# Three graph attention layers: partly filled columns of neighbours packed densely, their indices picked by one-hot products

## The chip, the cores and the metric

The kernel runs on one core of a Trainium2 chip. The metric is the device time of one execution in microseconds (us). The engines are PE (matrix products, with PEld loading weights), DVE (vector), ACT (activations), POOL (here it issues the indirect DMAs) and SP (issues ordinary DMAs, and runs in order). A wait is named by the engine that waits and by what ended it.

## What is computed

There are 6250 nodes with 256 features and 100000 edges from `src` to `dst`. Layers 1 and 2 are attention layers with 4 heads of 64, layer 3 one with 8 heads of 32. For each node the layer looks at the nodes that have an edge to it (and in layers 1 and 2 at the node itself):

```python
# layers 1 and 2 (xl, xr are x @ Wl, x @ Wr per head)
e = leaky_relu(xl[src] + xr[dst], 0.2); logits = einsum('ehc,hc->eh', e, att)
alpha = softmax of logits over the edges of each dst
out = segment_sum(xl[src] * alpha, dst) + b
# layer 3
e = leaky_relu(s1[src] + s2[dst], 0.2); out = segment_sum(softmax(e) * Wh[src], dst)
```

Between layers 1 and 2 stands an elu; behind layers 2 and 3 stand a residual sum and a layer norm.

## The kernel before

**Plan** (`make_plan`, L735): counts the edges of each node, sorts the nodes by degree, writes for each node the list of its sources next to its features to DRAM (`near_d`), and makes layer 1's table xl, one row of 260 numbers per node (`tables`). The lists are built on DVE in halves: `laid`, `shifted`, `filled` for the first nine of 17 segments, then for the other eight. The weights of layer 1 and of layer 2 are prepared here too (`left`, `right`; ACT L829, L833, DVE L842, L846). Seven indirect DMAs into a tile `spare` (L1254) have no reader.

**Blocks and columns.** The sorted nodes form 49 blocks of 128, a node to a partition, the highest degrees first. Block b has `cols[b]` columns: 27 in block 0, 25 in block 1, falling to 9 in block 48, 803 in all. Column j holds the j-th source of each node of the block. `columns` (L53) fixes these counts from the numbers of edges and nodes alone, with a margin, so that a last column may hold few real sources; the other lanes then point to a row "nobody" that weighs nothing. A column costs one indirect DMA on POOL (`gather_rows`, L1438), which brings 128 rows from the layer's table in DRAM into a column of a row tile. A row tile holds nine columns (T); there are nine of them (ROWS), so three blocks at most are in flight. `chunks` cuts a block into two to four row tiles (with a column for the node itself in layers 1 and 2).

**Packs.** Ten last columns share three gathers per layer: the packs are the blocks [3, 13, 17, 36], [26, 40, 47, 48] and [31, 43]. Each block has a fixed range of lanes in its pack. `pick_rows` (L1405, SP) copies the source indices into a column `pick` with small DMAs, `gather_pack` (L1410, POOL) gathers, `lay_rows` (L1418, SP) copies a block's share from the pack's tile into its row tile, and `lack_rows` (L1426, SP) fills the lanes below with nobody's row. So there are 796 gathers of columns and packs in a layer.

**Layers 1 and 2** are one function, `layer2` (L1702). For a block, `attend` computes on DVE z = max(g, xr) (the first chunk is made one block ahead, L1797, the others L1777), z times `at` (L1800), and the sum per head (L1801) into `lg`. `weights` takes the maximum (L1579, once per block, which marks blocks in the trace), the exponentials on ACT (L1587) and the normalisation on DVE. `weighted_sum` multiplies the rows by their weights, the last `few` columns on ACT with four instructions per column (L1629), the others on DVE (L1633), and PE adds the rows up by products with the identity (L1640). A row tile is free once PE has read it. `turns` transposes on PE (L1558, copied by ACT at L1563) and multiplies by weights (`product`, L1568): in layer 1 this makes `pr`, the block's own part for z, whose padding DVE sets at L1884, and the rows of layer 2's tables. `few` is `min(S // 3, last chunk - 1)` in layer 1 and `(2 * S - 2) // 3` in layer 2, with S = cols + 1.

**Order.** `layer2` starts with `begins(0..2)`, `find_few`, `gather(0)`, `turns(0)`, `fetch(1)`, `turns(1)`; then for each block b: `attend(b)`, the end of block b-1, `weighted_sum(b)`, `fetch(b + 2)`, `turns(b + 2)`. `begins(b)` in layer 1 is `start1` (L1887): an indirect DMA on POOL that brings a block's lists and features (`near_r` from `near_d`). `fetch(b)` calls `begins(b + 2)`; where block b + 2 opens a pack, it also calls `begins` of all the pack's blocks, and one block later `pick_rows`. With the packs above, four of these are at block 1 (3, 13, 17, 36). Then come the block's gathers, in order, on POOL. The order is written by hand; each engine runs its instructions in this order.

**Layer 3** is a loop behind them: per block, DVE alone computes `lg` (L2010), the weights, the products (L1662) and their sum (L1674). The gathers of block b + 1 are issued ahead of block b, and the result goes out by an indirect DMA on POOL (L2040).

Of the kernel before, what the change touches and what calls it, by code (L numbers as in the profile page):

```python
# [36 lines left out]
P = 128  # L37
# [10 lines left out]
def columns(E, N, NB):  # L48

    mean = E / N
    pmf = [math.exp(-mean)]
    for k in range(1, 200):
        pmf.append(pmf[-1] * mean / k)
    over, sd = [], []
    for c in range(199):
        p = sum(pmf[c + 1 :])  # L60
        g = sum((k - mean) * pmf[k] for k in range(c + 1, 200))
        over.append(N * p)
        sd.append(math.sqrt(max(N * (p * (1.0 - p) - g * g / mean), 0.0)))
    cols = []
    for b in range(NB):
        most = P * b
        cols.append(next(
            c for c in range(199) if (over[c] + 3.5 * sd[c] <= most if b else over[c] < 0.01)
        ))
    low = max((c for c in range(199) if N - over[c] <= P // 4), default=0)  # L70
    high = next(c for c in range(199) if over[c] <= P // 4)
    pmf += [0.0] * 200
    held = next(
        c for c in range(199)
        if N * sum((k - c) * pmf[k] for k in range(c, 200))
        + 3.5 * math.sqrt(N * sum((k - c) ** 2 * pmf[k] for k in range(c, 200))) <= P
    )
    assert cols[1] <= held < cols[0]
    part = {}
    for b in range(len(EARLY), NB):  # L80
        c = cols[b] - 1
        n = max(8, -(-int(math.ceil(over[c] + 3.5 * sd[c] - P * b)) // 8) * 8)
        if n < P:
            part[b] = n
    packs, taken = [], set()
    for b in sorted(part):
        if b in taken or part[b] > P * 3 // 4:
            continue
        pack, at = [], 0
        for k in range(b, NB):  # L90
            if k in part and k not in taken and at + part[k] <= P:
                pack.append((k, at, part[k]))
                at += part[k]
        if len(pack) > 1:
            packs.append(pack)
            taken.update(k for k, _, _ in pack)
    return cols, low, high, held, packs
# [569 lines left out]
def kernel(  # L667
# [22 lines left out]
    cols, low, high, held, packs = columns(E, N, NB)  # L690
# [7 lines left out]
    node_i = plan.tile([P, NB], I32, name="node_i")  # L698
    fits = plan.tile([P, 1], I32, name="fits")
# [11 lines left out]
    with tc.manual_schedule():  # L711
        make_plan(
            tc, x, src, dst, ((wl1, wr1, att1), (wl2, wr2, att2)), (b1, b2), w3, a3,
            cols, low, high, held, packs, node_i, fits, ident, eps, nobody, att, wc, wh, fixed, xl1_d,
            near_d,
# [6 lines left out]
    with tc.If(ok != 0):  # L722
        with tc.manual_schedule():
            tile_by_degree(
                tc, x, att1, b1, b2, w3, a3, out, [held] + cols[1:], packs, node_i, near_d, ident, eps, nobody,
                xl1_d, att, wc, wh, fixed, done,
            )
# [8 lines left out]
def make_plan(  # L736
    ctx, tc, x, src, dst, layers, biases, w3, a3, cols, low, high, held, packs, node_i, fits, ident, eps,
    nobody, att, wc, wh, fixed, xl1_d, near_d,
# [36 lines left out]
    SPARE = 7  # L775
# [23 lines left out]
    def filled_tile(name, shape, value, dtype=F32):  # L799
# [9 lines left out]
        for _ in layers  # L809
# [184 lines left out]
    for pack in packs:  # L994
        for b, _, n in pack:
            nc.gpsimd.tensor_scalar(
                most[:, b : b + 1], part_of, float(n), float(cols[b] - 1), op0=OP.is_lt, op1=OP.add
            )
# [25 lines left out]
    tables(8)  # L1024
    load(0, "r")
    for what in "lar":
        load(1, what)
# [79 lines left out]
    tables(1)  # L1107
    ohf = oh.rearrange("p k b -> p (k b)")
# [12 lines left out]
    tables(1)  # L1121
    for c0, c1 in cuts:
# [103 lines left out]
    no = one.tile([P, NB, CM], I32, name="no")  # L1226

    def filled(k0, k1):
        shape = [P, k1 - k0, CM]
        nc.vector.tensor_tensor(  # L1230
            no[:, k0:k1, :], ranks[:, None, :].to_broadcast(shape),
            count[:, k0:k1].unsqueeze(2).to_broadcast(shape), op=OP.is_ge,
        )
# [8 lines left out]
    HALF_S = (SEGS + 1) // 2  # L1242
    spans = [(k, min(NB, k + 9)) for k in range(0, NB, 9)]
    assert any(k0 == HALF_S * STEP for k0, _ in spans)
# [6 lines left out]
    spare = one.tile([P, SPARE, LONG], I32, name="spare")  # L1251
    left(1, nc.gpsimd)
    for k in range(SPARE):
        nc.gpsimd.indirect_dma_start(  # L1254
            out=spare[:, k, :], out_offset=None, in_=listed,
            in_offset=bass.IndirectOffsetOnAxis(ap=begin_i[:, k : k + 1], axis=1),
        )
# [12 lines left out]
    counts = one.tile([P, NB], F32, name="counts")  # L1270
# [12 lines left out]
    shifted(HALF_S, SEGS)  # L1283
    for k0, k1 in spans:
        if k0 >= HALF_S * STEP:
            filled(k0, k1)
# [6 lines left out]
    right(1)  # L1293
# [3 lines left out]
def tile_by_degree(  # L1297
    ctx, tc, x, att1, b1, b2, w3, a3, out, cols, packs, node_i, near_d, ident, eps, nobody,
    xl1_d, att, wc, wh, fixed, done,
# [7 lines left out]
    T = 9  # L1307
# [44 lines left out]
    late = consts.tile([P, len(EARLY)], F32, name="late")  # L1352
# [23 lines left out]

    def last_weights():
# [16 lines left out]
    packed = {b: (q, r, n) for q, pack in enumerate(packs) for b, r, n in pack}  # L1394
    opens = {pack[0][0]: q for q, pack in enumerate(packs)}
    shuts = {pack[-1][0]: q for q, pack in enumerate(packs)}
    picks = [consts.tile([P, len(packs)], I32, name=f"pick{k}") for k in range(2)]
    for pick in picks:
        nc.gpsimd.memset(pick, NP)
    held_rows = {}  # L1400

    def pick_rows(q, pick, of):

        for b, r, n in packs[q]:
            nc.sync.dma_start(pick[r : r + n, q : q + 1], of[:n, b, cols[b] - 1 : cols[b]])  # L1405

    def gather_pack(b, pool, name, pick, table, width):
        q = opens[b]
        held_rows[q] = pool.tile([P, RW], F32, name=name)
        nc.gpsimd.indirect_dma_start(  # L1410
            out=held_rows[q][:, :width], out_offset=None, in_=table,
            in_offset=bass.IndirectOffsetOnAxis(ap=pick[:, q : q + 1], axis=0),
        )

    def lay_rows(b, rows, width):

        q, r, n = packed[b]
        nc.sync.dma_start(rows[-1][:n, rows_at[b], :width], held_rows[q][r : r + n, :width])  # L1418

    rows_at = {}  # L1420

    def lack_rows(b, rows, cut, table, width):

        n = packed[b][2]
        rows_at[b] = cut[-1][1] - cut[-1][0] - 1
        nc.sync.dma_start(  # L1426
            rows[-1][n:, rows_at[b], :width],
            bass.AP(tensor=table.tensor, offset=table.offset + NP * width, ap=[[0, P - n], [1, width]]),
        )

    def gather_rows(b, rows, cut, own, table, of, width, j0, j1):


        for g, (s0, s1) in zip(rows, cut):
            for j in range(max(s0 - own, j0), min(s1 - own, j1)):
                if j + 1 == cols[b] and b in packed:
                    continue
# [88 lines left out]
    def sort_sources(work, ps, b):  # L1526

        n = cols[b]
# [19 lines left out]
        if b + 1 == len(EARLY):  # L1548
            pb = ps.tile([P, b + 1], F32, name="pb", tag="tp")
# [148 lines left out]
    def layer2(i, table, of, width, start, own, finish, follow):  # L1698
# [5 lines left out]
        with ExitStack() as es:  # L1704
# [5 lines left out]
            packp = es.enter_context(tc.tile_pool(name=f"pack{i}", bufs=len(packs)))  # L1710
# [5 lines left out]
            def gather(b):  # L1716
                first = EARLY[b] if b in begun else 0
                rows, cut = begun.pop(b) if first else row_tiles(b, 1)
                if b in opens:
                    gather_pack(b, packp, "pack", picks[i], table, width)  # L1720
                gather_rows(b, rows, cut, 1, table, of, width, first, cols[b])
                if b in packed:
                    lack_rows(b, rows, cut, table, width)
                    if b in opens:
                        waiting.append(lambda: lay_rows(b, rows, width))
                    else:
                        lay_rows(b, rows, width)
# [4 lines left out]
            waiting = []  # L1732
# [6 lines left out]
            def fetch(b):  # L1739
                if b + 2 < NB:  # L1740
                    begins(b + 2)
                if i == 0 and b + 2 in opens:
                    for k, _, _ in packs[opens[b + 2]]:
                        begins(k)
                if i == 0 and b + 1 in opens:
                    pick_rows(opens[b + 1], picks[0], sources)
# [35 lines left out]
            def attend(b):  # L1782
# [31 lines left out]
                few = min(S // 3, cut[-1][1] - cut[-1][0] - 1) if i == 0 else (2 * S - 2) // 3  # L1814
# [4 lines left out]
                if i == 0:  # L1819
# [3 lines left out]
                    if b in shuts:  # L1823
                        pick_rows(shuts[b], picks[1], spots)
# [15 lines left out]
            if i == 0:  # L1840
                find_few(work, pst)
            gather(0)
            turns(0, None)
# [5 lines left out]
            for b in range(NB):  # L1849
# [21 lines left out]
                if i == 0 and b == len(EARLY):  # L1871
                    load_last()
                if b + 2 < NB and not ahead(b):
# [102 lines left out]
    layer2(0, xl1_d[:, :], sources, W2 + 1, start1, own1, finish1, begin2)  # L1976
    last_weights()
    layer2(1, xl2_d[:, :], spots, W2, start2, own2, finish2, lambda: begin(0, wh_d, A1))

    with ExitStack() as es:  # L1980
        packp = es.enter_context(tc.tile_pool(name="pack3", bufs=len(packs)))
        work = es.enter_context(tc.tile_pool(name="work3", bufs=3))
        ps = es.enter_context(tc.tile_pool(name="ps3", bufs=3, space=PSUM))
        state = {}

        def gather(b):
            first = EARLY[b] if b in begun else 0
            rows, cut = begun.pop(b) if first else row_tiles(b, 0)
            if b in opens:
                gather_pack(b, packp, "pack3", picks[1], wh_d[:, :], A1)  # L1990
            gather_rows(b, rows, cut, 0, wh_d[:, :], spots, A1, first, cols[b])
            if b in packed:
                lack_rows(b, rows, cut, wh_d[:, :], A1)
                lay_rows(b, rows, A1)
# [4 lines left out]
        def attend(b):  # L1999
# [9 lines left out]
            for g, (s0, s1) in zip(rows, cut):  # L2009
# [3 lines left out]
                )  # L2013
            nc.vector.scalar_tensor_tensor(
# [101 lines left out]
```

## Time and profile before

| | us |
|---|---|
| median of nine runs (lowest, highest) | 3830.3 (3821.61, 3836.91) |
| the profiled execution | 3815.92 |
| its span | 3814.1 |
| DVE, POOL, PE, ACT busy in the span | 2720.9, 2487.0, 1610.8, 1337.8 |
| plan | 0 to about 104 |
| layer 1 | 104 to about 1426 |
| layer 2 | 1426 to about 2615 |
| layer 3 | 2615 to the end |

The stages are read off the first and last instructions of each stage's lines. A row of the groups reads: line, engine, operation, output from input, shape, count, then the busy time and the mean of one in ns, then the engine's idle time just ahead of these instructions and what ended most of it. In the timeline a row is start, duration, engine, line, operation, and in brackets the idle time ahead with its releaser. "issue" means that the profile shows nothing that was waited for.

### The profile page before, as it was taken

How to read it: one execution, taken by the hardware profiler on the slowest of the kernel's cores; microseconds unless marked ns; L12 is line 12 of the kernel's file. 1: busy time of each engine (PE TensorE's matmuls, PEld its weight loads, DVE VectorE, ACT ScalarE, POOL GpSimd, SP SyncE). 2: the span in 40 equal slices, each digit the busy share in tenths (PEclk: the TensorE clock that was granted, in tenths of full speed). 3: DMA queues.
4: the chain of work that ended last, by engine and by line, in shares of the span. 5: the costliest groups of instructions: out<-in, count | busy, mean ns of one | idle time of the engine just before them, and what ended most of it. 6: DMA issues, size and time to landing. Idle time of an engine off the chain costs nothing.

```text
span 3814.1 us, 25459 instructions
## 1 busy us (share of the span) xinstructions
PE 1610.8 (42%) x5423; PEld 1167.1 (31%) x5424; DVE 2720.9 (71%) x2609; ACT 1337.8 (35%) x5161; POOL 2487.0 (65%) x2587
## 2 busy tenths in 40 slices
PE   7336666465657764566665667664000000000000
PEld 6224545344545552343333445443000000000000
DVE  8648878566768886678876888894777566656665
ACT  3123434333434442566565667774000000000000
POOL 5666666665566645666666666664777777777774
PEclk8667878677778886678877887897555555555555
DMA  7433334333333433333433444442433333333332
GB/s 234 119 91 100 102 100 108 101 103 88 84 105 103 111 93 93 102 103 104 111 105 106 113 113 114 116 117 72 109 107 102 98 96 96 98 97 99 99 99 57
DMA packets 176463, 397.64 MB, mean 104 GB/s; under 512 B 50923, under 2 KB 93955, under 8 KB 176283
## 3 DMA queue, kind: packets, MB, share of 16 engines
q0 software_dynamic: 120608, 336.86, 32.8%
q1 hardware_dynamic: 53992, 57.08, 4.9%
q10 hardware_dynamic: 1700, 1.97, 0.2%
q8 instruction: 48, 0.79, 0.1%
q14 instruction: 115, 0.94, 0.1%
HBM read 354.60 MB, written 40.42 MB: 104 GB/s over the span
## 4 chain that ended last, share of the span: by engine, by line
issue 23%; POOL 19%; DVE 15%; ACT 14%; PE 10%; another core or an unknown queue 7%; DMA 2%; DVEq 0%; POOLq 0%; ACTq 0%; SPq 0%
POOL g L1438 18%; ACT g L1629 10%; PE acc L1640 7%; DVE z L1800 4%; DVE lg L1801 3%; DVE z L1797 2%; DVE z L1777 2%; ACT at L1587 2%; DVE g L1633 1%; POOL out L2040 1%; PE pm L1568 1%; DMA g<-xl_d,near_r 1%; PE pl L1568 1%; DVE weighted L1662 1%
## 5 line engine op out<-in xcount | busy, mean ns | idle before, releaser
L1438 POOL DMA_INDIRECT g<-xl_d,near_r x1549 | 1469.8, 949 | 823.8 <-issue 481.1
L1640 PE MATMUL acc<-g,ident 128*128 128x256 f32 x3408 | 1097.7, 477 | 789.6 <-issue 298.0
L1640 PEld LDWEIGHTS acc<-g,ident 128*128 128x128 f32 x3408 | 766.2, 237 | 1112.4 <-issue 371.9
L1438 POOL DMA_INDIRECT g<-whs_d,near_r x756 | 786.6, 1040 | 273.7 <-issue 244.0
L1629 ACT ACTIVATE g<-g,by 128x64 f32<-128x64 f32 x3080 | 803.9, 338 | 428.4 <-issue 417.3
L1801 DVE TENSOR_REDUCE lg<-z 128x28 f32<-128x1820 f32 (+4 forms) x234 | 497.3, 2125 | 8.4 <-DVE z L1800 0.3
L1800 DVE TENSOR_TENSOR z<-z,at 128x1820 f32<-128x1820 f32 (+4 forms) x234 | 496.8, 2123 | 4.7
L1674 DVE TENSOR_REDUCE acc_v<-weighted 128x256 f32<-128x3584 f32 (+10 forms) x47 | 319.0, 6787 | 22.3 <-remote 9.9
L1797 DVE TENSOR_TENSOR z<-g,pr 128x1820 f32<-128x1820 f32 (+3 forms) x138 | 299.6, 2171 | 17.4 <-DMA g<-xl_d,near_r 5.7
L1604 ACT ACTIVATE wt<-lg 128x128 f32<-128x128 f32 (+17 forms) x49 | 14.0, 285 | 801.8 <-DVE lg L1603 312.7
L1633 DVE TENSOR_TENSOR g<-g,at 128x256 f32<-128x256 f32 (+8 forms) x185 | 273.7, 1497 | 5.5 <-issue 1.1
L1563 ACT COPY xT<-pt 128x256 f32<-128x256 f32 x147 | 52.1, 373 | 512.4 <-PE pt L1558 251.5
L1662 DVE TENSOR_TENSOR weighted<-g,wt 128x1792 f32<-128x1792 f32 (+4 forms) x111 | 227.1, 2058 | 0.3
L1777 DVE TENSOR_TENSOR z<-g,pr 128x2080 f32<-128x2080 f32 (+4 forms) x96 | 197.9, 2061 | 36.8 <-remote 17.3
L2010 DVE TENSOR_TENSOR lg<-g,s_r 128x56 f32<-128x56 f32 (+4 forms) x111 | 22.4, 213 | 268.3 <-DMA g<-whs_d,near_r 247.7
L1884 DVE MEMSET pr<- 128x4 f32 x49 | 3.0, 62 | 239.5 <-PE pr L1568 168.7
L1587 ACT ACTIVATE at<-lg,top 128x19 f32<-128x19 f32 (+14 forms) x392 | 115.7, 295 | 138.5 <-issue 43.4
L1684 DVE BATCH_NORM_STATS2 stats<-acc 128x6 f32<-128x256 f32 x49 | 21.1, 430 | 146.7 <-PE acc L1640 87.1
L1568 PE MATMUL pm<-wcat,xT 128*128 128x260 f32 x392 | 107.9, 424 | 15.7 <-ACT xT L1563 15.7
L1568 PE MATMUL pl<-wcat,xT 128*128 128x260 f32 x196 | 77.8, 534 | 69.9 <-ACT xT L1563 66.8
L1568 PEld LDWEIGHTS pm<-wcat,xT 128*128 128x128 f32 x392 | 85.3, 218 | 33.2 <-ACT xT L1563 16.6
L1568 PE MATMUL pm<-wh_cat,xT 128*128 128x272 f32 x196 | 68.2, 478 | 52.4 <-ACT xT L1563 39.4
(267 smaller groups left out, 1751.4 us busy)
## 6 DMA issues: line engine op xcount, KB each, us to landing
g<-xl_d,near_r POOLq DMA_INDIRECT x1549
g<-whs_d,near_r POOLq DMA_INDIRECT x756
whs_d<-row SPq DMA_DIRECT2D x49, 132.0 KB
xl_d<-row SPq DMA_DIRECT2D x49, 130.0 KB
xr_d<-row SPq DMA_DIRECT2D x49, 130.0 KB
two<-xl_d SPq DMA_DIRECT2D x49, 130.0 KB
two<-xr_d SPq DMA_DIRECT2D x49, 130.0 KB
near_d<-x_all SPq DMA_DIRECT2D x7, 896.0 KB
```

The lines of the kernel that those rows point to most:

```text
L1438: nc.gpsimd.indirect_dma_start(out=g[:, j + own - s0, :width], out_offset=None, in_=table, in_offset=source(of, b, j),)
L1568: nc.tensor.matmul(pm, xT[:, c, :], w[:, c, :], start=c == 0, stop=c == 1)
L1587: nc.scalar.activation(wt[:, :, h], lg[:, :S, h], AF.Exp, bias=top[:, h : h + 1], accum_out=den[:, h : h + 1],)
L1629: nc.scalar.mul(g4[:, t, h, :], g4[:, t, h, :], by[:, s0 + t - a0, h : h + 1])
L1633: nc.vector.tensor_mul(g4[:, :m], g4[:, :m], wt[:, s0 : s0 + m, :].unsqueeze(3).to_broadcast([P, m, H, F // H]),)
L1640: nc.tensor.matmul(acc, ident, g4[:, t], start=False, stop=s0 + t == S - 1 and not more)
L1662: nc.vector.tensor_mul(prod[:, s0 - base : s1 - base, :].rearrange("p t (h d) -> p t h d", h=H), g[:, :n, :F].rearrange("p t (h d) -> p t ...
L1674: nc.vector.reduce_sum(part, prod[:, : s1 - base, :].rearrange("p s f -> p f s"), axis=AX.X)
L1777: nc.vector.tensor_max(z, rows[0][:, :n, :W2], xr[:, None, :].to_broadcast([P, n, W2]))
L1797: nc.vector.tensor_max(z, g[:, :n, :W2], xr[:, None, :].to_broadcast([P, n, W2]))
L1800: nc.vector.tensor_mul(z, z, at[:, None, :].to_broadcast([P, n, W2]))
L1801: nc.vector.reduce_sum(lg[:, s0:s1, :], z.rearrange("p t (h d) -> p t h d", h=H2), axis=AX.X)
```

## The change

**Packing.** `lanes_of` marks as partly filled each column that is expected (with a margin) to hold under 96 sources: 33 items (block, column), from (1, 23), (1, 24), (2, 22) to (48, 8). They have no gather of their own. All real sources of the items, in order, share one dense row of lanes, 14 packs of 128, and where an item begins is known only at run time. `base[b]` is the number of columns that remain, 770 in all, so a layer has 770 + 14 = 784 gathers, 12 fewer than before. Packs 0 to 2 are gathered at block 2, the others at blocks 4, 6, 8, 9, 16, 20, 21, 26, 35, 45 and 47 (`upon`). A pack's rows go into a tile, by SP to DRAM (`keep_packs`, 42 DMAs in all layers), and from there into the row tiles, from an offset that SP loads from memory (`lay_rows`: a load, a nop and a DMA, 33 per layer). `lack_rows` has 54 DMAs in all layers instead of 30. In layer 1 SP reads the packed indices of layer 2 and 3 back from DRAM (`pick_again`).

**Picks.** `find_lanes` runs once on DVE behind `find_few` (some 70 memsets, 27 comparisons and 15 other small instructions, one PE product). `pick_lanes` makes for each item a one-hot 128x128 and a 128x14 tile on DVE and adds their product on PE; 4 items at the start, 10 in `attend(0)`, the others a few at a time in `fetch`. `shut_lanes` is a DVE addition to `lg` in each block with items, in each layer (27 blocks).

**Order of the lists.** A pack can be picked only when the lists of all its blocks are there. `gather(b)` therefore calls `begins` for more blocks: after `gather(0)` 21 lists are begun when block 1's gathers start (7 before), 26 at block 2, 31 at block 4, 36 at 6, 40 at 7, all 49 at block 33.

**Plan.** The seven `spare` DMAs, and layer 2's weights, go. The second half of the lists is written in two parts (15 and then 17 segments), so the lists are written in three parts; a comparison for the last two spans is made earlier (`empty`). Layer 2's weights are prepared by `second_weights` between `gather(0)` and `turns(0)` of layer 1.

**Split.** `few` in layer 1 becomes `min(2 * S // 5, last chunk - 1)`: one more column on ACT in the 31 blocks or so with 18 columns or fewer, none more where the last chunk sets it.

```diff
 def make_plan(...)
-    left(1, nc.gpsimd)
-    for k in range(SPARE):
-        nc.gpsimd.indirect_dma_start(out=spare[:, k, :], ...)
...
-    shifted(HALF_S, SEGS)
-    for k0, k1 in spans:
-        if k0 >= HALF_S * STEP:
-            filled(k0, k1)
+    for q0, q1 in ((HALF_S, LAST_S), (LAST_S, SEGS)):
+        shifted(q0, q1)
+        for k0, k1 in spans:
+            if q0 * STEP <= k0 < q1 * STEP:
+                filled(k0, k1)
...
-    right(1)
 def tile_by_degree(...)
+    def pick_lanes(work, ps, lists):
...
+        for i in range(first, written[0]):
...
+            hot_l = work.tile([P, P], F32, name="lane_hot", bufs=2)
+            nc.vector.tensor_scalar(hot_l, numbers, lane_in[:, 0, i : i + 1], None, op0=OP.is_equal)
+            given = work.tile([P, K], F32, name="lane_given", bufs=2)
+            nc.vector.tensor_scalar(
+                given, numbers[:, 1 : K + 1], lane_in[:, 1, i : i + 1], lane_in[:, 2, i : i + 1],
+                op0=OP.is_equal, op1=OP.mult,
+            )
+            nc.tensor.matmul(pk, hot_l, given, start=i == first, stop=i + 1 == written[0])
+        nc.vector.tensor_add(pick_f, pick_f, pk)
...
-    def pick_rows(q, pick, of):
-        for b, r, n in packs[q]:
-            nc.sync.dma_start(pick[r : r + n, q : q + 1], of[:n, b, cols[b] - 1 : cols[b]])
...
+    def keep_packs(b, k):
+        for q in packs_at.get(b, ()):
+            nc.sync.dma_start(pack_d[k][q * P : (q + 1) * P, :], held_rows[q][:, : wide[k]])
...
     def lay_rows(...)
-        q, r, n = packed[b]
-        nc.sync.dma_start(rows[-1][:n, rows_at[b], :width], held_rows[q][r : r + n, :width])
+        for i in items_of.get(b, ()):
+            j = items[i][1] + own
+            g, s0 = next((g, s0) for g, (s0, s1) in zip(rows, cut) if s0 <= j < s1)
+            nc.sync.dma_start(g[: top[i], j - s0, : wide[k]], pack_d[k][lane(i), :])
...
+    def shut_lanes(b, lg, own, H):
+        if b in items_of:
+            i0, n = items_of[b][0], len(items_of[b])
+            s = lg[:, base[b] + own : cols[b] + own, :]
+            nc.vector.tensor_add(s, s, shut[:, i0 : i0 + n].unsqueeze(2).to_broadcast([P, n, H]))
...
 def layer2: gather(b)
+                if i == 0 and b:
+                    begun_lists[0] = min(NB, 1 + max(
+                        [b + 2] + [items[filled_by[q]][0] for q in range(K) if upon[q] <= b + 2]
+                    ))
+                    for k in range(begun_lists[0]):
+                        begins(k)
 def layer2: fetch(b)
-                if i == 0 and b + 2 in opens:
-                    for k, _, _ in packs[opens[b + 2]]:
-                        begins(k)
-                if i == 0 and b + 1 in opens:
-                    pick_rows(opens[b + 1], picks[0], sources)
+                if i == 0 and b > 1:
+                    pick_lanes(work, pst, begun_lists[0])
+                gather_packs(b, pack_tile, picks[i], table, width)
+                keep_packs(b, i)
 def layer2: attend(b)
+                shut_lanes(b, lg, 1, H2)
+                if i == 0 and b == 0:
+                    pick_lanes(work, pst, begun_lists[0])
-                few = min(S // 3, cut[-1][1] - cut[-1][0] - 1) if i == 0 else (2 * S - 2) // 3
+                few = min(2 * S // 5, cut[-1][1] - cut[-1][0] - 1) if i == 0 else (2 * S - 2) // 3
 def layer2: start
                 find_few(work, pst)
+                find_lanes(zp, pst)
+                pick_lanes(work, pst, 3)
             gather(0)
+            if i == 0:
+                second_weights()
```

## The prediction

> **What bounds the kernel now.** I read the 40 slices and the windows by stage first, then the waits of DVE and of POOL by stage, then the timeline of POOL at the places where it stops. Windows (start:end, then busy us of PE, PEld, DVE, ACT, POOL):
>
> ```profile
> 0.00:104.00 104.00, 82.39 (x418) 66.51 (x419) 77.97 (x157) 41.35 (x144) 51.10 (x96) 0.90 0.80 231
> 250.00:700.00 450.00, 286.34 (x1011) 219.78 (x1009) 376.64 (x330) 184.72 (x685) 291.01 (x308) 0.79 0.38 103
> 700.00:1426.00 726.00, 467.19 (x1626) 361.99 (x1626) 535.56 (x469) 290.63 (x1148) 429.02 (x453) 0.78 0.37 98
> 2615.00:3700.00 1085.00, 20.00 (x56) 12.69 (x56) 677.49 (x708) 68.70 (x205) 806.45 (x779) 0.50 0.36 98
> ```
>
> DVE is the busiest engine in layers 1 and 2 (73 to 84% of these stretches), POOL in layer 3. But POOL's share understates it. The rows of its timeline show 0.95 us busy and 0.30 us idle for each indirect DMA, thus 1.25 us per column when nothing holds it:
>
> ```profile
> 142.76 0.95 POOL L1887 DMA_INDIRECT near_r<-near_d,node_i  x1 [0.30 <-issue]
> 144.01 0.95 POOL L1887 DMA_INDIRECT near_r<-near_d,node_i  x1 [0.30 <-issue]
> ```
>
> In layer 1, block 10 (from one L1579 to the next) takes 27.0 us: DVE is busy for 23.1, POOL issues 19 to 20 DMAs, 24 to 25 us. Both are close, and both wait for the other through the nine row tiles. DVE's waits in layer 1, then its first one in layer 3:
>
> ```profile
> DVE pr L1884 <- PE pr L1568: 168.7, 22, 50.2
> DVE h L1910 <- ACT pos L1905: 17.9, 2, 14.8
> ...
> DVE z L1777 <- DMA g<-xl_d,near_r: 6.4, 5, 4.9
> ```
> ```profile
> DVE lg L2010 <- DMA g<-whs_d,near_r: 247.7, 32, 10.9
> ```
>
> In layer 1 DVE seldom waits for the gathers; it waits for `pr`, thus for PE and ACT behind them (`turns` stands behind the block's weighted sum). In layer 3 it waits for gathers in 32 blocks. There POOL issues 805 indirect DMAs in 1100.0 us, 1.37 each, until the last gather ends at 3766.3; from 3716 on DVE runs with long steps (21 us per block for 10.7 busy) and sets the end itself. POOL's stops for a pack in layer 1:
>
> ```profile
> 211.88 0.95 POOL L1410 DMA_INDIRECT pack<-xl_d,pick  x1 [0.30 <-issue]
> 223.25 0.95 POOL L1438 DMA_INDIRECT g<-xl_d,near_r  x1 [10.42 <-issue]
> ```
> ```profile
> 900.12 0.95 POOL L1410 DMA_INDIRECT pack<-xl_d,pick  x1 [19.78 <-DMA pick<-near_r]
> ```
>
> The first is a wait for a row tile just behind a pack, and would remain. The second, with one of 18.52 at 1019.4, is a wait for the pick; the blocks about them take 34.6, 34.9 and 41.6 us.
>
> **The change part by part**, against the profiled execution (3815.92; span 3814.1, so 1.8 lies around it).
>
> *Plan (ends at 103.6).* ACT's rows of layer 2's weights stand at 82.72 to 85.26, within the tables, which PE and ACT finish last (102.7, 1.1 us per block). Taking them out gives about 2.2. DVE is done at 95.93, so what it loses or the lists in three parts give comes into its own only through the last `near_d` DMA (issued 95.25), which the first list gather (103.32) doesn't wait for longest. The seven `spare` DMAs on POOL have no reader. Bounds 0 and -5; I take **-3**.
>
> *Start of layer 1.* Ahead of block 1's gathers four lists are begun now; 18 afterwards: 14 x 1.25 = 17.5 us on POOL. Ahead of block 2's there are 4 more (5.0), while the columns gone and the packs added nearly cancel. DVE gets `find_lanes`: 70 memsets (0.06 each, some 0.03 apart, about 2), 27 comparisons and 15 others at 0.15 to 0.24, 8.5; then 4 items at 0.76 (0.48 by the 128x128 comparison L1451, 0.28 for the small one by L1456, its nearest row), 3; then `second_weights`, 2. Of these 16, 4.72 + 2.48 = 7.2 lie in gaps ahead of the first z (119.31), so 9 are left; block 0's four chunks keep DVE busy from there to its last z at 143.88, so there is no later cover. Ten items in `attend(0)` add 7.6. DVE's 16.6 and POOL's 17.5 lie side by side: about +18. On top: between 107 and 212 POOL issued without a pause, and PE and ACT ran slowly. ACT's multiplications stand 1.40 us apart there (0.24 at 879 to 901, where POOL stands still), and DVE waits 50.2 for `pr`:
>
> ```profile
> 172.09 0.35 ACT L1629 ACTIVATE g<-g,by 128x64 f32<-128x64 f32 x1 [1.06 <-issue]
> 173.49 0.35 ACT L1629 ACTIVATE g<-g,by 128x64 f32<-128x64 f32 x1 [1.04 <-issue]
> ```
>
> With 22 us more of issuing, this stretch lasts longer. No row says by how much it sets the end; between +10 (all lost in the 50.2 wait that is there) and +45 (all of it added to 18) I take **+25**.
>
> *Rest of layer 1.* The lists fetched early are gone later: 18 x 1.25 = 22.5 less for POOL, and 11 columns less, 13.8: 36 together. Since issuing (24 to 25) is just over DVE (23.1) in such blocks and the rest of the period is a wait through the tiles, I count 70%: -25. (All of it: -36. None, if `pr` sets the pace: 0.) The two pick stops lengthen their blocks by some 25; afterwards DVE and PE make picks in `fetch`, one block ahead, at blocks 4, 6, 8, 9, 16, 20, 21, 26, 35, 45 and 47. What POOL waits there no row shows: from 0 to 19.8, the old stop, at four of them. I take 15 in all, so -10. DVE: 19 items x 0.76 = 14.4, 27 additions at 0.18 = 5, less 31 x 0.27 = 8 by `few`: +11, of which blocks past 39, DVE-bound (16.6 against 16.2), and the like feel +4. ACT: 31 blocks x 4 x 0.338 = 42, at steps of 0.70 it would be 87; ACT is busy under half of the time, yet its last multiplication stands ahead of PE's sum and `turns`: between -8 and +45, I take +6. Sum **-25**.
>
> *Layer 2.* 12 columns less: 15.0 if POOL set the pace. DVE waits there for PE's sum and ACT's exponentials (83.0 and 62.1 at its largest waits), not for gathers; 27 additions cost 5. **-3**, bounds -12 and +8.
>
> *Layer 3.* 12 x 1.37 = -16.4 if POOL sets the pace to the end. Eight of the columns fall before block 43 (11.0); behind it DVE sets the end, and five additions at its step of 1.4 come on top. Where a pack's rows go over DRAM they need two transfers and a load by SP: the one such load in the trace took 1.42 (L728), an SP copy of a share 0.69 to issue, and no row shows a landing of the whole chain. The packs stand first in their block's gathers, ahead of 9 to 20 columns of 1.37, which hide it except in the last blocks. **-10**, bounds -16 and +6.
>
> The Trainium skill ("DMA: Bandwidth & Descriptors", Anatomy of one DMA) puts a fixed cost of about 2.0 us on each DMA, mostly completion. By it the way over DRAM would be some 4 us behind the gather, twice the copy before; this speaks against the change wherever a pack's block is itself next in line. No row of before shows this way.
>
> Sum: -3 + 25 - 25 - 3 - 10 = **-16**, so 3799.9 for an execution like the profiled one. That one lies 0.38% below the median of the runs shown (3830.3), so I scale: 3799.9 x 3830.3 / 3815.92 = **3814**. About 0.2% (7.7 us) is what a measurement of this kernel can tell from no change.
>
> **The rivals.**
>
> *Larger gain.* Blocks 3 to 38 follow POOL wholly (-36), no stop for a pick is left (-25), the start costs 18, ACT and DVE hide: layer 1 -43. With -4, -6 and -14 elsewhere -67; halfway to the forecast, -45, is its centre: **3785**. For it: POOL issues 24 to 25 of 27.0. Against it: 168.7 of DVE's waits are for `pr`.
>
> *Slower: the lists in front.* 21 lists ahead of block 1 lengthen the stretch in which PE and ACT crawl, and nothing is given back since `pr`, not POOL, sets the pace of blocks 8 to 31. Start +45, rest of layer 1 only -10, plan, layers 2 and 3 together -10: +25, **3855**. For it: the 50.2 wait at 190.0, and 1.40 us steps under POOL's load. It decides if block 3's L1579 comes over 35 us later against before and blocks 8 to 31 shorten by less than 0.5 us each.
>
> *Off the path.* Layer 1's two terms cancel, layer 2 stays, layer 3's gain goes into its DVE-bound tail or into waits for packs: -3 in all, **3827**. A form of it: the packing saves columns as it says, but in layer 3 POOL waits for the tiles instead.
>
> **How the numbers follow.** Forecast 0.35 (from -8 to -32), larger gain 0.20, off the path 0.17, slower 0.28. Faster by over 0.2%: 0.35 + 0.20 = 0.55; within: 0.15; slower: 0.28 and the upper edge of off the path, 0.30. The range takes in half of the larger gain beyond its centre and all but the tail of the slower case: 3770 to 3860.
>
> **What would show it.** In the profile after: the first list gathers to 21 in one row without a gap up to about 165 us, block 1's first column there; the first z of layer 1 at about 128; block 3's L1579 some 25 late; blocks 8 to 31 some 1 to 2 us shorter each; no stop of POOL above 10 us ahead of a pack; layer 3 shorter by about 10, with its last gather some 12 earlier against its start. Wrong would be: stops of POOL or DVE of over 5 us ahead of several packs (the price of the way over DRAM, or of picks in DVE's order), layer 2 changed by over 12, or a start that costs nothing.

## The result, and the profile after

The changed kernel is slower: 3932.82 us (median of 14 runs) against 3827.62 (46 runs of the kernel before), a ratio of 1.0273, with 1.0254 to 1.0291 as its interval. Its profiled execution took 3928.34, its span 3926.5. The experiments ran in several series; each experiment's ratio is against the kernel before in the same series, on the same chip.

When DVE reaches a block's maximum (L1579 before, L1753 after) gives a table of where the time went:

| place | before | after | difference |
|---|---|---|---|
| layer 1, block 0 | 152.8 | 253.7 | +100.8 |
| block 3 | 307.3 | 390.1 | +82.8 |
| block 8 | 453.9 | 576.5 | +122.6 |
| blocks 20, 21 | 813.5, 838.6 | 919.0, 980.9 | +105.6, +142.3 |
| blocks 34, 35 | 1179.4, 1197.1 | 1289.0, 1339.0 | +109.6, +141.9 |
| block 47 | 1412.4 | 1532.8 | +120.4 |
| layer 2, block 48 | 2614.9 | 2731.4 | +116.5 |
| end of the span | 3814.1 | 3926.5 | +112.4 |

So, up to block 3, +82.8 comes from the start (with the plan in it), +37.6 from blocks 3 to 47 of layer 1, -3.9 from layer 2 and -4.1 from layer 3. Within the rest of layer 1 the difference grows by 40 from block 3 to 8, then falls slowly in most blocks and jumps at some: 20 to 21, 34 to 35, and once more at the last block, 48, to +145.3, which the start of layer 2 takes back (+119.9 at its block 0).

The stretch from 104 to 1412, at whose end layer 1 of the kernel before reached block 47, first in the kernel before, then two windows of the kernel after, the plan and the same stretch (at its end it had reached block 39); the columns are as in the prediction's windows:

```profile
104.00:1412.00 1308.00, 785.19 (x2721) 603.08 (x2722) 968.07 (x863) 487.82 (x1880) 808.51 (x853) 0.76 0.37 100
```
```profile
0.00:104.00 104.00, 81.47 (x418) 65.96 (x419) 77.01 (x158) 38.44 (x126) 40.57 (x77) 0.90 0.78 224
104.00:1412.00 1308.00, 659.95 (x2411) 508.43 (x2411) 885.68 (x1024) 451.00 (x1736) 736.19 (x776) 0.73 0.35 93
```

In this stretch all four engines are idler now, DVE with 161 more instructions. The loss is waiting. DVE's timeline in `find_lanes`, in the kernel after:

```profile
134.20 0.21 DVE L1490 TENSOR_SCALAR z<-numbers,counts 128x1 f32<-128x1 f32 x1 [1.07 <-issue]
135.60 0.21 DVE L1490 TENSOR_SCALAR z<-numbers,counts 128x1 f32<-128x1 f32 x1 [1.19 <-issue]
136.31 0.21 DVE L1490 TENSOR_SCALAR z<-numbers,counts 128x1 f32<-128x1 f32 x1 [0.50 <-issue]
137.00 0.21 DVE L1490 TENSOR_SCALAR z<-numbers,counts 128x1 f32<-128x1 f32 x1 [0.47 <-issue]
```

Each comparison works for 0.21 and starts 0.70 or 1.40 after the last, with nothing waited for. POOL issues indirect DMAs beside it all the time. `find_lanes` lasts from 110.3 to 193.9. Then POOL's side, in its timeline:

```profile
163.12 0.95 POOL L2078 DMA_INDIRECT near_r<-near_d,node_i  x1 [0.30 <-issue]
...
254.51 0.95 POOL L1567 DMA_INDIRECT two<-xl_d,pick  x1 [61.62 <-DVE pr L2075]
```

The 18 lists stand in front without a gap, as forecast, and then POOL waits 61.62 for the first picks, which DVE makes at the end of block 0. Such waits go on. POOL's and DVE's waits in layer 1 of the kernel after (engine, line, what ended it, us in total, times, longest):

```profile
POOL two L1567 <- DVE pick L1555: 133.2, 7, 32.0
POOL two L1567 <- DVE pr L2075: 61.6, 1, 61.6
```
```profile
DVE pick_f L1552 <- PE lane_k L1551: 78.7, 11, 15.0
```

Two new waits: POOL for picks ahead of a pack (147 at nine packs behind block 2: the 133.2 above and two stops of 13.7 put down to PE), and DVE for the product of its one-hot tiles on PE. How the second arises is seen in DVE's timeline of a block:

```profile
488.56 0.29 DVE L1547 TENSOR_SCALAR lane_given<-numbers,lane_in 128x14 f32<-128x14 f32 x1
498.02 0.17 DVE L1552 TENSOR_TENSOR pick_f<-pick_f,lane_k 128x14 f32<-128x14 f32 x1 [9.17 <-PE lane_k L1551]
498.23 0.15 DVE L1555 CAST pick<-pick_f 128x1 int32<-128x1 f32 x1
498.30 2.04 DVE L1985 TENSOR_TENSOR z<-z,at 128x1820 f32<-128x1820 f32 x1
```

`fetch` stands behind `weighted_sum`, so on PE the small product is queued behind all of the block's sums. DVE's addition waits for it, and behind the addition stands the next block's work, z times `at` (L1985).

### The profile page after: what moved, and what is told of

Its sections match the earlier page's. It is cut to its first block, busy times and chain, and to the rows that moved or that the text cites. A ratio compares the mean times of both kernels' runs of the same rounds, so it can differ in the third digit from the quotient of the medians.

```text
span 3926.5 us, 26745 instructions
## 1 busy us (share of the span) xinstructions
PE 1565.3 (40%) x5491; PEld 1139.3 (29%) x5492; DVE 2757.8 (70%) x2948; ACT 1363.1 (35%) x5274; POOL 2435.1 (62%) x2530
## 5 line engine op out<-in xcount | busy, mean ns | idle before, releaser
L1612 POOL DMA_INDIRECT g<-xl_d,near_r x1503 | 1425.6, 948 | 785.8 <-issue 439.9
L1814 PE MATMUL acc<-g,ident 128*128 128x256 f32 x3408 | 1075.8, 470 | 888.6 <-issue 323.4
L1814 PEld LDWEIGHTS acc<-g,ident 128*128 128x128 f32 x3408 | 752.7, 233 | 1207.1 <-issue 388.3
L1803 ACT ACTIVATE g<-g,by 128x64 f32<-128x64 f32 x3192 | 829.5, 337 | 421.4 <-issue 401.4
L1612 POOL DMA_INDIRECT g<-whs_d,near_r x733 | 758.9, 1035 | 255.1 <-issue 226.6
L1985 DVE TENSOR_TENSOR z<-z,at 128x1820 f32<-128x1820 f32 (+4 forms) x234 | 496.8, 2123 | 4.7
L1848 DVE TENSOR_REDUCE acc_v<-weighted 128x256 f32<-128x3584 f32 (+10 forms) x47 | 319.0, 6787 | 26.9 <-remote 12.3
L1807 DVE TENSOR_TENSOR g<-g,at 128x256 f32<-128x256 f32 (+7 forms) x185 | 266.2, 1456 | 4.8 <-DVE at L1774 1.6
L1567 POOL DMA_INDIRECT two<-xl_d,pick x14 | 13.3, 947 | 209.7 <-DVE pick L1555 133.2
L1742 PE MATMUL pm<-wcat,xT 128*128 128x260 f32 x392 | 95.4, 387 | 1.4 <-ACT xT L1737 0.9
L2239 POOL DMA_INDIRECT out<-y,node_i x49 | 52.9, 1079 | 66.6 <-ACT y L1870 44.7
```

Source lines behind the costliest of these rows:

```text
L1612: nc.gpsimd.indirect_dma_start(out=g[:, j + own - s0, :width], out_offset=None, in_=table, in_offset=source(of, b, j),)
L1742: nc.tensor.matmul(pm, xT[:, c, :], w[:, c, :], start=c == 0, stop=c == 1)
L1803: nc.scalar.mul(g4[:, t, h, :], g4[:, t, h, :], by[:, s0 + t - a0, h : h + 1])
L1807: nc.vector.tensor_mul(g4[:, :m], g4[:, :m], wt[:, s0 : s0 + m, :].unsqueeze(3).to_broadcast([P, m, H, F // H]),)
L1814: nc.tensor.matmul(acc, ident, g4[:, t], start=False, stop=s0 + t == S - 1 and not more)
L1848: nc.vector.reduce_sum(part, prod[:, : s1 - base, :].rearrange("p s f -> p f s"), axis=AX.X)
```

## The experiments

Each experiment stands here with what was expected of it before it ran, and with its result. Theories: **A**, DVE's small instructions at the start are given out slowly because POOL issues beside them; **C**, picks come late, for POOL (a pack reached before its pick) and for DVE (the product behind PE's sums). Rivals: **B**, these instructions are slow by themselves; **D**, POOL would wait for row tiles anyway.

### Start and picks, each mended

```diff
             find_lanes(zp, pst)
             pick_lanes(work, pst, 3)
+            held_up = consts.tile([P, 1], F32, name="held_up")
+            nc.gpsimd.tensor_copy(held_up, pick_f[:, :1])
         gather(0)
```

e1, POOL held until the first picks are made:

> The changed kernel, with one copy on POOL that reads the picks' sum ahead of gather(0): POOL issues no column of block 0 until find_lanes and the first four items are through. Theory A (DVE's small instructions are given out every 0.70 to 1.40 us while POOL issues indirect DMAs, as from 110 to 194 in the profile after): with POOL still they take 10 to 20 us in all, block 0's L1753 comes at 165 to 185 instead of 253.7 although its gathers start later, and the time falls by 60 to 90, to 3845 to 3875. Rival B (the 85 memsets and 28 comparisons on one tile, and the round trips over PE, are slow by themselves): they end at about 205 as before, the gathers start behind them, and the time is 3930 to 3970.

3903.6 (one run), 29 less than the kernel after. DVE's timeline of this kernel:

```profile
107.27 1.95 DVE L1487 MEMSET z<- 128x1 f32 x85
109.15 3.52 DVE L1490 TENSOR_SCALAR z<-numbers,counts 128x2 f32<-128x2 f32 x28
```

With POOL still, `find_lanes` takes 9.2 (107.3 to 116.5) instead of 83.6: B falls, and A holds for `find_lanes`. But block 0's maximum comes at 201.6, not at 165 to 185: POOL now issues beside the ten picks of `attend(0)`, which from 168 on take 4.2 us each, 35.8 in all. In the kernel after, where POOL stood still beside them (its wait of 61.62), the ten took 6.6. So holding POOL moved a part of the loss from `find_lanes` to these picks; most of DVE's idle time among them is put down to something the trace doesn't name.

```diff
+            find_lanes(zp, pst)
             for b in range(3):
                 begins(b)
             find_few(work, pst)
-            find_lanes(zp, pst)
```

e2, `find_lanes` first:

> The changed kernel with find_lanes ahead of the first lists (begins) and of find_few, where POOL has nothing to issue; only the four first items stay behind find_few. Theory A: find_lanes takes 10 to 15 us, mostly in DVE's gap ahead of find_few; block 0's L1753 at 160 to 180, time 3840 to 3865. Rival B: find_lanes still takes 60 us or more, the lists and gathers wait for little of it, block 0's L1753 stays past 230, time over 3900.

3893.8 (one run). Neither: the gathers started at 111.5, only 1.5 behind `find_lanes`, so it took 39.5 (110.0 to 149.5), and block 0's maximum came at 217.2.

The next edit, shortened:

```diff
 def attend(b):
     while behind:
         behind.pop()()
+    add = pick_lanes(work, pst, begun_lists[0])   # returns the addition
     first_z(b + 1)
+    add()
 def fetch(b):
-    pick_lanes(work, pst, begun_lists[0])
```

e3, picks in `attend`:

> The changed kernel with the start as it is, but the picks made in attend(b) of the same lists, ahead of the block's multiplications (on PE ahead of its sums), and their addition put behind the first z of the next block. Theory C (DVE's addition L1552 waits for a PE product queued behind the block's sums, 78.7 us, and POOL waits for it ahead of seven packs, 133.2 us): both waits fall under a quarter, layer 1 from block 3 on is 30 to 45 us shorter, time 3885 to 3900. Rival D (POOL would wait there for row tiles anyway, and the pick is only what ends last): the waits move to row tiles, the time changes by under 10.

3907.4 (one run), 25 less. From block 3 to 47 it gained 42 on the kernel after, as C asked; but block 3 was reached 9 later (`find_lanes` took 94.7). DVE's wait for the product fell from 78.7 to 29.7, but POOL still stops for a pick at four packs (14.2, 11.5, 18.8 and 17.7), so C's waits didn't all fall as far as it asked. D gets none of its case.

e4, e2 and e3 together:

> Both edits together: find_lanes ahead of the lists, picks in attend. A and C: the two gains add, 3933 - 80 - 40 = about 3810, 0.2 to 0.8% under the kernel before. B and D: over 3900.

3873.49, ratio 1.0125 (1.0061 to 1.0189). The two gains add, to about half of what both theories asked for.

### The price of the parts alone

In the kernel before, n memsets of one column behind `find_few`, n = 16 and 85:

e5, 16 memsets:

> The kernel before with 16 one-column memsets on DVE between find_few and gather(0), into a tile that z uses later. Theory A in its finer form (some 20 to 30 instructions that DVE's sequencer holds ready run at full speed, those behind come at the slow step while POOL issues): free, block 0's L1579 within 3 us of 152.8, time within 10 of before. A coarser A (every instruction under POOL's load costs 0.7 to 1.4): 11 to 22 us later.

e6, 85 memsets:

> The kernel before with 85 such memsets. Work on DVE: 85 at about 0.02 apart, 1.9 us (107.3 to 109.15 with POOL held). Theory A: as in the changed kernel (110.3 to 127.9 there), 15 to 25 us; block 0's L1579 at 163 to 180, time 10 to 25 over before. Rival B' (it is find_lanes' dependences and comparisons that are slow, not the number of instructions): under 4 us, time as before.

With 16: 3812.8 against one run of 3820.7, with block 0 at 158.4, 5.6 later, which its first list gather was too; with 85: 3842.9 against the same. DVE's timeline with 16, then the first rows with 85:

```profile
117.61 0.28 DVE L1844 MEMSET z<- 128x1 f32 x16
```
```profile
114.21 0.30 DVE L1844 MEMSET z<- 128x1 f32 x19
115.00 0.06 DVE L1844 MEMSET z<- 128x1 f32 x1 [0.48 <-issue]
115.70 0.08 DVE L1844 MEMSET z<- 128x1 f32 x2 [0.65 <-issue]
...
152.32 0.06 DVE L1844 MEMSET z<- 128x1 f32 x1 [1.48 <-issue]
```

The first 19 go at full speed, and the last of the other 66 starts at 186.7: 72.5 us for 85 instructions that need 2. This looks like a store of some twenty that run freely, and a slow supply behind it; the rows show the pace only, and that there is such a store, of fetched instructions or others, is argued, not shown. More was lost at block 0 than expected (+72.5), yet only +31.6 was left at block 3 and 22 in the time: block 2's long wait for `pr`, 50.2 in the kernel before, was 9.0 here and took up the rest.

In the kernel before, `for k in range(21): begins(k)` in `fetch(1)`, in one run and, in another series, in ten:

e7, 21 lists in front, one run:

> The kernel before with the lists of blocks 0 to 20 begun in fetch(1), as the changed kernel does, so 15 more indirect DMAs ahead of block 1's columns, and 15 fewer later. The prediction's rival (lists in front cost the start 18 to 45 and nothing comes back since pr sets the pace): time 10 to 40 over before. The term that was forecast (18 in front, most of it back by block 33): within 8 of before.

e11, the same, ten runs:

> The kernel before with the lists of blocks 0 to 20 begun in fetch(1), again, timed. From its first look (3806.5 against one run of 3820.7): ratio 0.996 to 0.999. The rival, that lists in front cost: over 1.002.

3806.5 against one run of 3820.7; in ten runs the ratio is 1.0001 (0.9982 to 1.0019): the first run's gain was scatter. In the first run block 1 came 20.1 later, block 24 3.0, block 42 0.2. In the profile of the ten, from a series in which the kernel before too was slower than in its own profile, it is 22.4, 10.9 and 16.7. So the lists cost some 20 in front; that all of it comes back is shown by the ratio, to within some 7 us, and where it comes back by one profile only. As a whole they cost nothing, and the rival of the prediction falls.

DMA traffic without POOL (copies of the table by SP, in the kernel of e1), and other work of POOL (80 memsets ahead of the hold):

e8, copies by SP:

> The first experiment again (POOL held until the picks), with four copies of half the table each, DRAM to DRAM, 13 MB in all, issued by SP ahead of find_lanes: DMA traffic without POOL. If it is POOL's issuing that slows DVE's dispatch, find_lanes still takes 9 us from its first memset to L1516; if it is the load on the DMA engines and the memory (about 100 GB/s under the gathers), it takes 40 us or more. The time says nothing here (the copies delay the rest).

e16, memsets on POOL:

> The first experiment (POOL held until the picks) with 80 memsets of 128x128 on POOL ahead of the hold, beside find_lanes: POOL is busy, but issues no DMA. If it is the issuing of indirect DMAs that slows DVE's dispatch: find_lanes takes 9 to 12 as with POOL held. If any work of POOL does: 40 or more.

`find_lanes` took 9.2 in e8 and 9.5 in e16. The window of the copies, and the window of the slow comparisons in the kernel after (the last number is GB/s):

```profile
105.00:120.00 15.00, 3.90 (x16) 3.25 (x16) 11.75 (x152) 0.27 (x1) 0.00 (x0) 0.50 1.02 348
```
```profile
128.00:165.00 37.00, 0.00 (x0) 0.00 (x0) 5.96 (x30) 0.00 (x0) 28.11 (x30) 0.50 0.43 114
```

Three times the traffic does no harm, and neither do POOL's memsets. Of what was tried, only POOL's indirect DMAs go with the slow steps.

In the kernel before, `few = min(2 * S // 5, ...)` alone:

e12, ACT's share:

> The kernel before with only ACT's share in layer 1 at 2 * S // 5. The prediction's terms: DVE -8 in part, ACT +6: within 0.2%. If ACT's multiplications set the pace under POOL's issuing (steps of 0.70): 20 to 60 over, ratio 1.005 or more.

0.9991 (0.9969 to 1.0013): no difference.

### A version with all mends, and the mends taken back

The edits, shortened:

```diff
+    second_loads()           # layer 2's weights, loads only
     find_lanes(zp, pst)
     for b in range(3): begins(b)
+    nc.gpsimd.tensor_copy(held_up, late[:, len(EARLY):])
     find_few(work, pst)
     gather(0)
     second_weights()         # the rest
 gather(b): lists begun
-    ... if upon[q] <= b + 2]
+    ... if upon[q] <= b + 2 + (b > 1)]
 attend(b): picks as in e3, all of them, three items per DVE instruction
```

e9, all mends:

> The changed kernel mended where the runs so far showed its costs: find_lanes first, and gather(0) held until it is through; the loads of layer 2's weights ahead of it; from block 2 on lists begun one block earlier; all picks in attend, three items per DVE instruction, their addition behind the first z of the next block. If dispatch under POOL's issuing and late picks are the whole of the loss: block 0's L1753 at 160 to 175, no wait of POOL for a pick over 8 after block 2, time 3790 to 3815, 0.2 to 0.9% under the kernel before. If something else of the change costs (shares over DRAM, the fetch of lists, ACT's share): still over 3830.

e10, all mends, with ACT's share as before the change:

> The same with ACT's share in layer 1 as before (S // 3). If the larger share costs ACT what the prediction allowed (6 in 42), 3 to 10 less than the run above; if DVE's 8 less counts, 3 to 8 more; within 3 if neither sets the pace.

Ratios 0.9935 (0.9900 to 0.9969) for e9 and 0.9894 (0.9863 to 0.9926) for e10, medians 3817.75 and 3800.29: both beat the kernel before, by 0.6 and 1.1%. Behind block 2 POOL waits for no pick in either (1.6 once, in e9). DVE still waits 35.6 ahead of `pick_f` in e10, so that part of the loss isn't mended there. e10 is 17 less than e9, more than was expected, but their intervals overlap, so the share of ACT is not settled here; alone it did nothing.

Back from e10, first the hold, then the earlier lists:

e13, e10 without the hold:

> The mended kernel with ACT's share as before (e10), without the hold: POOL issues block 0's columns beside find_lanes. Theory A: find_lanes takes 40 to 85 instead of 10, block 0's L1777 at 210 to 240 instead of 168; of this some half is taken up by block 2, as in the run with 85 memsets: 15 to 40 over e10, 3815 to 3840. If the hold doesn't matter: within 8 of e10.

e14, e10 without the earlier lists:

> The mended kernel (e10) with the lists from block 2 on begun as late as in the changed kernel, so the picks of a pack a block later. Theory C: POOL again waits 10 to 18 for a pick at four packs (20, 21, 26, 35), the time is 15 to 40 over e10. Rival D (it waits for row tiles anyway): within 8.

Without the hold: 0.9948 (0.9927 to 0.9970). `find_lanes` took 43 and block 0 came 27 later (195.1 against 168.0), but block 1 was nearly where it was (252.5 against 250.5), for it needs the first packs, gathered at 223.9 against 221.9. About 0.5% or 20 us, at the edge of the intervals. Without the earlier lists: 1.0131 (1.0096 to 1.0166), 2.4% more. POOL's waits for picks are back at packs 20, 26 and 35 (13.1, 16.9, 14.2; 4 to 8 at three earlier ones), each of the three with an echo in the next blocks' row tiles (10.4, 18.3, 11.3); between blocks 3 and 47 of layer 1 the mended kernel gains 61.5 on the kernel before, this one loses 8.7 to it. D falls.

The mended start alone, in the changed kernel:

e15, the start's mends only:

> The changed kernel with the mended start alone (find_lanes first, gather(0) held, loads of the weights early); picks as in the changed kernel, item by item, in attend(0) and in fetch. With e4's and e9's results: the start is worth 40 to 70 of the 105 lost: 3865 to 3895. If it is worth all, 3830 or less; if under 20, the picks are the cause.

1.0199 (1.0156 to 1.0241): 28 of the 105. Block 0 came 38 earlier than in the kernel after, block 47 by 29. From block 3 to 47 it loses 41.1 to the kernel before, about what the kernel after loses (37.6): the rest of layer 1 doesn't hang on the start.

Then the picks' part alone, with the start as changed: the lists one block earlier (one line), and that with the picks in `attend`:

e17, lists one block earlier:

> The changed kernel with one edit: from block 2 on, the lists of a pack (and so its picks, still made in fetch) are begun one block earlier. Theory C (a pick that POOL reaches before DVE has made it is the larger part of the loss): POOL's waits ahead of packs after block 2 fall from 147 to under 50, layer 1 is 40 to 70 shorter, time 3860 to 3890; the 79 that DVE waits for the picks' products on PE stay, and the start stays. If the place within the block matters more than the block: 3905 to 3925.

e18, e17 with the picks in `attend`:

> The same, with the picks in attend, item by item, as in e3, and the start of the changed kernel (find_lanes behind find_few, nothing held). The whole of the picks' mend without the start's: no wait of POOL for a pick after block 2, 3815 to 3845. What is left over the mended kernel (3800 and 3818) is the price of the start, 10 to 30 as in e13 and e15.

Ratios 1.0131 (1.0114 to 1.0148) for e17 and 0.9938 (0.9921 to 0.9954) for e18. In this series all kernels were faster, the kernel before at 3236.6 (3235.7 to 3237.9, seven runs), and the slow steps were not there: `find_lanes` took 9.2 beside POOL's issuing. So these two show C without A. DVE's waits and POOL's, with the lists earlier only:

```profile
DVE pick_f L1552 <- PE lane_k L1551: 72.4, 11, 10.7
```
```profile
POOL two L1567 <- DVE pick L1555: 15.9, 2, 12.7
```

POOL's wait has gone (15.9 of 133.2), DVE's has stayed (72.4 of 78.7), and the kernel is still 42 slower than before. In the other both are gone (2.5 for the product, nothing for picks), and it is 62 faster than its neighbour, 20 faster than before. So of the 86 that the two waits lose by this one edit (69.9 and 15.9) 62 come off the time: most of what DVE waits for the product stands on the path.

## Why the prediction was wrong

Step by step, as it was put:

- **Plan, -3**: not told apart. The first list gather came at 99.95 instead of 103.32, but with the same plan at 99.3 and 107.4 in e1 and e2, and in kernels with the plan of before at 105.9 and 109.0 (e6, e5).
- **Start, +25**: failed, +82.8 at block 3 with the plan's share in it. The lists cost about the 17.5 to 22.5 that were worked out, and nothing in the end (e11). The term for DVE failed: some 10.5 us for the 112 small instructions of `find_lanes` (with the first four items and layer 2's weights, 16), priced by their work, when the profile of before showed ACT's multiplications 1.40 apart beside POOL's issuing. The row was read as a matter of PE and ACT and not applied to DVE's new instructions. With POOL still they took 9.2 (e1), so the price was right for that company; beside POOL's issuing they took 83.6. The count was off too: 85 memsets, not 70.
- **Its weight**: the mended start took back 38 of the 100 at block 0, and 28 of these are in the time (e15). Block 3 is still 50 later than before there, and 57 in e10, where `find_lanes` takes 10.1 and block 0 is only 15 late. Some 20 of this are the lists; in e10 DVE stands 30.2 among the picks of `attend(0)`, ahead of the first packs, which the sum had at 7.6 for ten items. How the rest divides was not taken apart, so a start at the forecast's +25 was not reached by any run.
- **Rest of layer 1, -25**: failed, +37.6. The columns saved are worth what was counted, and more: with picks in time for POOL blocks 3 to 47 are 61.5 shorter (e10), or 45.1 (e9), against 25 forecast and both bounds together of 61 (36 for the columns and lists, 25 for the old stops). Each is one profile; in those of e11 and e12, whose times did not change, the same stretch differs from before by -4.9 and +12.3. The step that failed is "one block ahead ... I take 15 in all": POOL runs a block ahead of DVE, so a pick one block ahead in the program is not ahead: 147 at nine packs instead of 15, and with the lists later alone the mended kernel loses 2.4% (e14). Its own sign of being wrong, stops of over 5 us ahead of several packs, is what came. And a wait that the working left out, of DVE for PE: it named nothing queued behind `L1552`, where the next block's z times `at` stands. DVE waited 78.7 there.
- **Layer 2, -3**: -3.9; no run takes its terms apart, so that they held is not shown. **Layer 3, -10**: -4.1, inside its bounds. Up to block 40 it gained 15 (+116.5 to +101.4); blocks 41 to 46 gave 15 back (+116.6), the last two took 11 off again, and the end behind them added 6. DVE's waits ahead of `den` (L2061 before, L2260 after), put down to "issue" or to something the trace doesn't name, rose from 36.2 to 52.5 in this layer. The tail was taken for DVE-bound from about block 43 or 44 on; in the kernel after the long steps (21 to 24 us per block) began at block 41.
- **ACT's share**: within noise (e12), as far as it was tried alone.
- **The rival that ends slower** had the right sign and the wrong mechanism: not the lists in front, but slow small instructions and picks behind time. Its test (block 3 over 35 late, blocks 8 to 31 shorter by under 0.5 each; they were by 0.4) came true for other reasons.
- **The sums**: "halfway to the forecast" for the larger gain is -41.5, not -45, so its centre would be 3789; the forecast doesn't hang on it.

The Trainium skill ("DMA: Bandwidth & Descriptors", Anatomy of one DMA) was cited for the way over DRAM at some 4 us; that section gives its 2.0 us for DMAs that GpSimd issues, and here SP issues them. No experiment took that way out, so its price is not shown; with the way in place e10 and e18 beat the kernel before. The skill also says ("Runtime: NRT & Kernel Launch", Instruction fetch mechanics) that each sequencer fetches its next block itself, by a DMA queue of its own, and that this is mostly hidden. It is not hidden here if the steps are fetches. From 105 to 200 the kernel after has three packets on an instruction queue, against some 65 gaps of over 0.4 on DVE, so the steps aren't one packet on that queue each.

Open: what in POOL's indirect DMAs goes with the slow steps of the others, and why they were absent in the last series, on a chip that had shown them in the series before (`find_lanes` of e13: 43). Whether the kernel after would beat the one before there was not tried; with its lists one block earlier it did not.

## What to carry to other kernels

A value that one engine makes for another must be ahead of the engine that runs ahead, not of the program: look how many blocks the issuing engine leads, and put the work there. A reduction of DMAs is worth its count only if no engine waits in order for what feeds it; look at what is queued behind each waiting instruction, on both sides. And price small instructions by how far apart they start in the same company, not by their work: here the one-column memsets started 0.02 apart alone, and mostly 0.70 to 1.40 beside indirect DMAs.

## What the hardware showed that was not expected

DVE's small instructions started at steps of about 0.70, 1.40 or 2.10 us while POOL issued indirect DMAs: 85 memsets in 72.5 us, the first 16 to 19 of them in 0.3 (e5, e6). Neither 348 GB/s of copies nor POOL's memsets did this (e8, e16). In one series the steps were absent: the same kernel before took 3236.6 instead of 3835.4 and 3829.8 in the two series ahead of it. In that series ACT's multiplications started 0.24 or 0.25 apart in 949 of 989 steps between 250 and 1100 (e18); in the kernel after 121 of 647 steps there were of 1.40. And layer 3's indirect DMAs came every 1.26 us on average (e18), against 1.39 in the profile of the kernel before.
